# A third buffer for the second layer's input, an earlier load, and a moved stage plan

## Chip, cores and metric

The kernel runs on one core of one Trainium2 chip. The metric is device microseconds of one execution. Engines are named as the profile names them: PE (TensorE), PEld (its weight loads), DVE (VectorE), ACT (ScalarE), POOL (GpSimd) and SP (SyncE), whose only work here is to issue DMA transfers. All data are float32.

## What is computed

Two residual layers over `x` of 8 batches, 1024 tokens and 512 channels, conditioned by `cond` (8 x 1024). Cut to what matters:

```python
# layer 0: modulated attention, 16 heads of 32
xn  = layernorm(x * s1)                      # s1, s2: the halves of cond
q, k, v = xn @ Wq.T * q_dc, xn @ Wk.T * k_dc, xn @ Wv.T * v_dc * s2
out = softmax(q @ k.T * scale) @ v
x   = x + out @ Ww.T * w_dc + v @ Wu.T * u_dc

# layer 1: gated state-space scan, 1024 inner channels, 16 states
xr, gate = split(x @ W_in.T)                 # 1024 columns each
xr  = xr + cond
xc  = silu(causal_conv4(xr) + b_conv)        # depthwise over tokens, 4 taps
xn  = (xc - mean) / sqrt(var + 1e-5) * ln_g + ln_b
Bm, Cm, dt = split(xn @ W_xproj.T)           # 16 columns each
Ad  = 1 - tanh(dt @ W_dt.T + b_dt) * 0.01 * tanh(A_log)
Bd  = Bm * min(norm(xn), 1)
for t in range(1024):                        # h: 8 x 16 x 1024
    h = clip(h * Ad[t] + Bd[t] * xn[t], -10, 10)
    y[t] = Cm[t] @ h
x   = x + ((y + D * xn) * silu(gate)) @ W_out.T
```

## The kernel before

**The whole.** `modulated_attention` does layer 0 and leaves its result in a DRAM scratch `x1_d`, cut into 32 chunks of 32 tokens (512 KB a chunk, all batches). `gated_scan` does layer 1. All instructions stand in each engine's queue in the order in which Python emits them (`manual_schedule`), and every engine works through its own queue in that order, waiting on semaphores.

**The scan.** State `h` is one tile of 128 partitions (8 batches x 16 states) by 1024 channels. One token is one `step`: a single custom DVE instruction (L805) that adds the token's weighted input and clamps. Its input is `xb`, the normalised row of the token repeated over the 16 states. It is made by DMA: `spill` writes the normalised tile `xt` (16 tokens, 512 KB) to a DRAM scratch `xd` (L623), and `fetch` reads 4 tokens of it back with 8 broadcast transfers (one a batch, 256 KB landed each, L771). The pool `xbp` holds three such groups of four tokens. `weigh` (ACT, L781) multiplies a token's `xb` by its weight `ws` two steps before its `step`. `products` (PE, L792) sums the states for four tokens into `y`.

**The plan.** Everything else of the layer is cut into small stages and hung on the steps by hand. `at(n, f, ...)` says that stage `f` is emitted right after step `n`. For chunk `c`, `p0 = 32*(c-1)`, so its stages at `p0 - 22` to `p0 + 31` come before its own first step at `p0 + 32`, and those up to `p0 + 84` after it. In a steady stretch every window of 32 steps holds stages of four chunks. Below, "place k" is what is emitted after step k of such a window (k from 0 to 31, so a stage at `p0 - 9` is at place 23). Within a place, earlier chunks come first, then stages in the order of the `at` lines, then `fetch`, `products` and `weigh`.

**The stages of one chunk**, in the order in which its data passes them:

- `load_x1` (SP, L435): the chunk's 512 KB from `x1_d` into `x1`, from a pool of two buffers. A buffer is free when `order(1)` (ACT, L699) of the chunk two back has read it.
- `begin` (ACT): carries three tokens of conv history over.
- `conv_mm` (PE, L546, L550), `conv_in` (ACT, L557, L559), `conv_taps` (DVE, L566), `conv_out` (ACT, L573): input product, conv and silu, eight times, once for each 128 channels, a new one every second step.
- `flip_mm` (PE), `stats`, `center`, `deviation`, `scale` (mostly DVE): transposes and layer norm, for each half of the chunk (tile 0 and tile 1, 16 tokens each); then `spill` (SP) and `squares` (ACT). `skip` (DVE, L636) later scales the same `xt` in place by `D`, so it waits until the spill has read it.
- `p_mm`, `p_out`, `p_flip`, `lengths`, `params`, `params_mm`, `params_out`: the projections Bm, Cm, dt. `spread` (POOL, L667) sends them with 8 small transfers to the 128 partitions as `bca`; `decay` (ACT tanh L671, then DVE) makes the weights `ws` and the clamp limits from them, `weights` (DVE) the matrices for `products`.
- `order`, `gate_mm` (PE, L704), `gate` (ACT, L712), `add_y`, `gate_y` (DVE, L717, L721), `out_flip`, `out_copy`, `out_mm` (PE, L738, L744), `out_store` (ACT), `out_send` (POOL, L759): the gate and the output product.

**Queues.** SP's queue holds, for one chunk, 64 transfers of `fetch`, two of `spill` and one of `load_x1`. In the built program they take turns on eight semaphores: each SP transfer also waits until the transfer eight places ahead of it in the queue has landed. All matrix results of the layer share four PSUM buffers (tag `mm`), two more hold `y`.

Of the kernel before, what the change touches and what calls it, by code (L numbers as in the profile page):

```python
# [8 lines left out]
F32 = mybir.dt.float32  # L9
# [6 lines left out]
P = 128  # L16
B = 8
H = 512
KH = H // P
# [3 lines left out]
KI = DI // P  # L23
NS = 16
TC = 32
# [3 lines left out]


@with_exitstack
def modulated_attention(ctx, tc, const, x1_d, xu_d, S, x, xT, cond, wT, ident, sT):

# [5 lines left out]
    nc = tc.nc  # L41
# [3 lines left out]
    SB = 2 * NQ  # L45
    NAMES = ("q", "k", "v", "w", "u")

    eps = const.tile([P, 1], F32, name="eps_h")
    nc.vector.memset(eps, EPS)
    dc = const.tile([P, 5, KH, B], F32, name="dc")  # L50
    xp = ctx.enter_context(tc.tile_pool(name="xh", bufs=3))
    tok = ctx.enter_context(tc.tile_pool(name="tok", bufs=2))
    small = ctx.enter_context(tc.tile_pool(name="small", bufs=6))
# [59 lines left out]
    with tc.tile_pool(name="w0", bufs=2) as wp:  # L113
        s2T = wp.tile([P, 2 * KH, B], F32, name="s2T")
        nc.scalar.activation(s2T, sT, AF.Square)
        for n, name in enumerate(NAMES):
            w = wp.tile([P, KH, H], F32, name="w")
# [21 lines left out]
    two = ctx.enter_context(tc.tile_pool(name="two", bufs=2))  # L139
# [259 lines left out]
def gated_scan(ctx, tc, const, x1_d, S, w_in, w_conv, cols, ln_g, ln_b, w_x, w_xd, w_dt, b_dt, a_log,  # L399
# [10 lines left out]
    nc = tc.nc  # L410
# [3 lines left out]
    NX = 3 * NS  # L414

    wp = ctx.enter_context(tc.tile_pool(name="w1", bufs=1))
    one = ctx.enter_context(tc.tile_pool(name="s1", bufs=1))
    two = ctx.enter_context(tc.tile_pool(name="s2", bufs=2))
    hp = ctx.enter_context(tc.tile_pool(name="hp", bufs=6))
    xcp = ctx.enter_context(tc.tile_pool(name="xcp", bufs=2))  # L420
    xtp = ctx.enter_context(tc.tile_pool(name="xtp", bufs=4))
# [6 lines left out]
    def load(ap, name, shape):  # L428
        t = wp.tile(shape, F32, name=name)
        nc.sync.dma_start(out=t, in_=ap)  # L430
        return t

    def load_chunk(c):
        x1 = two.tile([P, KH, B, TC], F32, name="x1")
        nc.sync.dma_start(  # L435
            out=x1.rearrange("p k b t -> p (k b t)"), in_=x1_d[c].rearrange("p k b t -> p (k b t)")
        )
        return x1

    win_sb = wp.tile([P, KH, 2 * DI], F32, name="win")  # L440
    nc.sync.dma_start(out=win_sb[:, :, 0:DI], in_=w_in[:, 0:DI].rearrange("(k p) o -> p k o", p=P))
    x1_now = load_chunk(0)
    cw = load(w_conv.rearrange("(k p) j -> p k j", p=P), "cw", [P, KI, 4])
    cb = load(cols["b_conv"], "cb", [P, KI])
    lg = load(cols["ln_g"], "lg", [P, KI])
    lb = load(cols["ln_b"], "lb", [P, KI])
    g_bc = load(ln_g.unsqueeze(0).to_broadcast([P, DI]), "g_bc", [P, DI])
    b_bc = load(ln_b.unsqueeze(0).to_broadcast([P, DI]), "b_bc", [P, DI])
    d_bc = load(d_skip.unsqueeze(0).to_broadcast([P, DI]), "d_bc", [P, DI])
# [6 lines left out]
    nc.sync.dma_start(out=wx_sb[:, :, 0 : 2 * NS], in_=w_x.rearrange("(k p) o -> p k o", p=P))  # L456
    wxd = xtp.tile([NS, DI], F32, tag="xt", name="wxd")
    nc.sync.dma_start(out=wxd, in_=w_xd)
    wdt = load(w_dt, "wdt", [NS, NS])
    my_sb = load(mask_y, "mask_y", [P, B])  # L460

    few = wp.tile([P, 4 * CW], F32, name="few")
# [6 lines left out]
    eps = wp.tile([P, 1], F32, name="eps_i")  # L469
    nc.vector.memset(eps, EPS)  # L470
    nc.scalar.activation(na, na, AF.Tanh)
    nc.vector.tensor_scalar_mul(na, na, -0.01)
    zero = wp.tile([P, TC], F32, name="zero")
    nc.vector.memset(zero, 0.0)

# [21 lines left out]
    pts = []  # L499
    for n in range(2):  # L500
        pt = wp.tile([P, 2 * NS + P], F32, name=f"pt{n}")
        nc.vector.memset(pt, 0.0)
        pts.append(pt)
    yws = []
    for n in range(2):
        yw = wp.tile([P, TT, 4 * B], F32, name=f"yw{n}")
# [23 lines left out]
    def at(n, f, *args):  # L530
        plan.setdefault(n, []).append(lambda: f(*args))
# [4 lines left out]
    def load_x1(st, c):  # L536
        st["x1"] = load_chunk(c)
# [106 lines left out]
    def params(st, i):  # L644
        rs = st["rs", i]
        pt = st["p", i] = pts[i][:, 0:NX]
        add = two.tile([P, NX], F32, name="p_add")
        nc.vector.scalar_tensor_tensor(add, wgs, rs[:, 1:2], wb, ALU.mult, ALU.add)
        nc.vector.scalar_tensor_tensor(pt, st["pt_ps"][:, i, 0:NX], rs[:, 0:1], add, ALU.mult, ALU.add)
        nc.vector.tensor_scalar_mul(pt[:, 0:NS], pt[:, 0:NS], st["nr"][:, i : i + 1])  # L650
# [161 lines left out]
    for c in range(NCH):  # L812
        st, n0 = sts[c], c * TC
        p0 = n0 - TC
        if c > 0:
            at(p0 + -15, load_x1, st, c)
        at(p0 + -15, begin, st)
        for k in range(KI):
            at(p0 + -9 + 2 * k, conv_mm, st, k)
            at(p0 + -8 + 2 * k, conv_in, st, k)  # L820
            at(p0 + -7 + 2 * k, conv_taps, st, k, (0, 1))
            at(p0 + -6 + 2 * k, conv_taps, st, k, (2,))
            at(p0 + -5 + 2 * k, conv_out, st, k)
        at(p0 + 11, flip_mm, st, 0, 0)
        at(p0 + 11, flip_mm, st, 0, 1)
        at(p0 + 12, stats, st, 0, 0)
        at(p0 + 12, stats, st, 0, 1)
        at(p0 + 12, center, st, 0)
        at(p0 + 13, deviation, st, 0)
        at(p0 + 14, scale, st, 0)  # L830
        at(p0 + 15, spill, st, 0)
        at(p0 + 17, squares, st, 0)
        at(p0 + 23, skip, st, 0)
        at(p0 + 14, flip_mm, st, 1, 0)
        at(p0 + 14, flip_mm, st, 1, 1)
        at(p0 + 15, stats, st, 1, 0)
        at(p0 + 15, stats, st, 1, 1)
        at(p0 + 15, center, st, 1)
        at(p0 + 16, deviation, st, 1)
        at(p0 + 17, scale, st, 1)  # L840
        at(p0 + 22, spill, st, 1)
        at(p0 + 18, squares, st, 1)
        at(p0 + 28, skip, st, 1)
        at(p0 + 15, p_mm, st)
        at(p0 + 19, p_out, st)
        at(p0 + 20, p_flip, st)
        at(p0 + 18, lengths, st)
        at(p0 + 22, params, st, 0)
        at(p0 + 23, params_mm, st, 0)
        at(p0 + 24, params_out, st, 0)  # L850
        at(p0 + 20, params, st, 1)
        at(p0 + 21, params_mm, st, 1)
        at(p0 + 24, params_out, st, 1)
        at(p0 + 25, spread, st)
        at(p0 + 29, decay, st)
        at(p0 + 30, weights, st, 0)
        at(p0 + 36, weights, st, 1)
        at(p0 + 31, order, st, 0)
        at(p0 + 38, gate_mm, st, 0, 0)
        at(p0 + 40, gate, st, 0, 0)  # L860
        at(p0 + 41, gate_mm, st, 0, 1)
        at(p0 + 42, gate, st, 0, 1)
        at(p0 + 51, add_y, st, 0)
        at(p0 + 56, gate_y, st, 0)
        at(p0 + 59, out_flip, st, 0, 0)
        at(p0 + 60, out_copy, st, 0, 0)
        at(p0 + 62, out_mm, st, 0, 0)
        at(p0 + 60, out_flip, st, 0, 1)
        at(p0 + 62, out_copy, st, 0, 1)
        at(p0 + 65, out_mm, st, 0, 1)  # L870
        at(p0 + 68, out_store, st, 0)
        at(p0 + 70, out_send, st, c, 0)
        at(p0 + 48, order, st, 1)
        at(p0 + 51, gate_mm, st, 1, 0)
        at(p0 + 54, gate, st, 1, 0)
        at(p0 + 54, gate_mm, st, 1, 1)
        at(p0 + 58, gate, st, 1, 1)
        at(p0 + 65, add_y, st, 1)
        at(p0 + 73, gate_y, st, 1)
        at(p0 + 75, out_flip, st, 1, 0)  # L880
        at(p0 + 76, out_copy, st, 1, 0)
        at(p0 + 78, out_mm, st, 1, 0)
        at(p0 + 75, out_flip, st, 1, 1)
        at(p0 + 77, out_copy, st, 1, 1)
        at(p0 + 79, out_mm, st, 1, 1)
        at(p0 + 81, out_store, st, 1)
        at(p0 + 82, out_send, st, c, 1)
    for g in range(S // 4):
        at(4 * g - 9, fetch, g)
        at(4 * g + 4, products, g)  # L890
# [13 lines left out]
@with_exitstack  # L904
def network(ctx: ExitStack, tc: tile.TileContext, S, ins, out):
    nc = tc.nc
    const = ctx.enter_context(tc.tile_pool(name="const", bufs=1))
    dram = ctx.enter_context(tc.tile_pool(name="dram", bufs=1, space=DRAM))
    x1_d = dram.tile([S // TC, P, KH, B, TC], F32, name="x1_d")
    xu_d = dram.tile([2, H, S], F32, name="xu_d")  # L910
    ident = const.tile([P, P], F32, name="ident")
    nc.sync.dma_start(out=ident, in_=ins["ident"])
    sT = const.tile([P, 2 * KH, B], F32, name="sT")
    nc.sync.dma_start(out=sT, in_=ins["condT"].rearrange("(k p) b -> p k b", p=P))
    with tc.manual_schedule():
        modulated_attention(
            tc, const, x1_d, xu_d, S, ins["x"], ins["xT"], ins["cond"], {n: ins[f"w{n}T"] for n in "qkvwu"}, ident, sT
        )
        gated_scan(
            tc, const, x1_d, S, ins["w_in"], ins["w_conv"],  # L920
            {n: ins[f"{n}_c"] for n in ("b_conv", "ln_g", "ln_b")}, ins["ln_g"], ins["ln_b"],
            ins["w_x"], ins["w_xd"], ins["w_dt"], ins["b_dt"], ins["a_log"], ins["d_skip"],
            ins["w_out"], ident, ins["cond_k"], ins["mask_y"], out,
        )
# [65 lines left out]
```

## Time and profile before

| | |
|---|---|
| median of 3 runs | 6010.15 us (6007.41 to 6031.06) |
| the profiled execution's own time | 6021.71 us |
| its span, first to last instruction | 6019.9 us |
| layer 0 | about 0 to 3465 us |
| second layer's constants and first chunk | about 3465 to 3549 us |
| scan, first to last step | 3549 to 5997 us |
| busy in the whole span | PE 94%, DVE 74%, ACT 64%, POOL 26% |
| granted TensorE clock, mean | 0.98 |

The engines' rows of the profile give busy time; idle time before an instruction is put down to what released it. DMA share is the mean busy share of the core's 16 DMA engines. A queue line of SP shows when a transfer was issued, not when it landed.

### The profile page before, as it was taken

The numbers are of one execution on the slowest core, as the hardware profiler recorded it, in microseconds if no ns is written. First come the engines' busy times: TensorE is split into PE (matmuls) and PEld (weight loads), VectorE is DVE, ScalarE is ACT, GpSimd is POOL, SyncE is SP. The second block draws the span as 40 slices with busy tenths as digits, with TensorE's granted clock in tenths as the row PEclk, the third lists the DMA queues.
The fourth block names the chain that finished last, engine by engine and source line by source line (L and its number), as shares of the span: only waits on it lengthen the run. The fifth ranks groups of instructions, "written<-read, shape, count | busy, mean of one in ns | idle before, by whom it ended". The sixth has DMA issues, their size and how long they took to land.

```text
span 6019.9 us, 113426 instructions
## 1 busy us (share of the span) xinstructions
PE 5660.1 (94%) x42960; PEld 3310.4 (55%) x42960; DVE 4469.2 (74%) x6917; ACT 3846.8 (64%) x6743; POOL 1549.8 (26%) x1668
## 2 busy tenths in 40 slices
PE   7999999999999999999999879999999999999998
PEld 5555555555555555555555545555555555555553
DVE  2666666766666666667666569999989998989997
ACT  3655555655655555556555358877777777777786
POOL 2433433433433434334333201101111111111111
PEclk8999999999999999999999989999999999999999
DMA  2102212111112022121111279999989999899997
GB/s 71 38 17 64 52 41 64 29 57 50 37 48 66 21 59 59 34 64 37 51 37 36 63 203 252 248 244 248 249 239 246 248 250 243 241 242 247 241 249 207
DMA packets 387648, 781.81 MB, mean 130 GB/s; under 512 B 203664, under 2 KB 285840, under 8 KB 354336
## 3 DMA queue, kind: packets, MB, share of 16 engines
q1 hardware_dynamic: 358432, 756.07, 46.2%
q0 software_dynamic: 28672, 18.48, 1.4%
q8 instruction: 342, 5.60, 0.4%
q14 instruction: 202, 1.65, 0.1%
HBM read 663.62 MB, written 83.89 MB: 124 GB/s over the span
## 4 chain that ended last, share of the span: by engine, by line
PE 51%; DMA 27%; DVE 8%; ACT 8%; SPq 4%; issue 2%; POOL 0%; ACTq 0%; DVEq 0%; POOLq 0%
DMA xb<-xd 24%; PE mm_ps L153 16%; PE t_ps L262 13%; PE s_ps L252 9%; PE mm_ps L269 8%; DVE h L805 4%; SPq L771 4%; ACT pr L370 3%; ACT pT L367 2%; PE in_ps L546 1%; DMA xd<-xt 1%; ACT xb L781 1%; DVE xt L604 1%; PE y_ps L792 1%; PE o_ps L744 1%
## 5 line engine op out<-in xcount | busy, mean ns | idle before, releaser
L360 DVE TENSOR_REDUCE nmax<-s_ps 128x1 f32<-128x1024 f32 x1024 | 1206.1, 1220 | 478.2 <-PE s_ps L255 477.6
L367 ACT COPY pT<-t_ps 128x512 f32<-128x512 f32 x1024 | 550.1, 589 | 1377.7 <-PE t_ps L262 1377.4
L805 DVE CUSTOM_DVE_ANT_0 h<-h,xb,lim 128x1024 f32<-128x1024 f32 x1024 | 1372.9, 1341 | 64.4 <-ACT xb L781 21.0
L262 PEld LDWEIGHTS t_ps<-ident,pr 128*128 128x128 f32 x8192 | 910.0, 141 | 647.0 <-issue 451.3
L781 ACT ACTIVATE xb<-xb,ws 128x1024 f32<-128x1024 f32 x1024 | 1152.4, 1146 | 174.6 <-DMA xb<-xd 151.8
L370 ACT ACTIVATE pr<-s_ps,nmax 128x1024 f32<-128x1024 f32 x1024 | 1140.3, 1128 | 5.7 <-DVE nmax L360 5.5
L262 PE MATMUL t_ps<-ident,pr 128*128 128x128 f32 x8192 | 1095.9, 277 | 30.8 <-ACT pT L367 28.5
L546 PE MATMUL in_ps<-x,win 128*128 128x256 f32 x2048 | 530.2, 405 | 88.0 <-DMA x<-x_d 88.0
L389 POOL TENSOR_SCALAR pr<-pr,rinv 128x1024 f32<-128x1024 f32 x512 | 575.2, 1123 | 144.7 <-DVE rinv L388 140.8
L252 PE MATMUL s_ps<-kT,qT 32*128 32x512 f32 x2048 | 601.0, 641 | 4.4 <-ACT pr L370 4.4
L255 PE MATMUL s_ps<-k,q 32*128 32x512 f32 x2048 | 578.0, 640 | 0.0
L759 POOL DMA_DIRECT2D out<-o_sb x256 | 150.5, 594 | 1642.5 <-ACT xr L557 824.3
L375 POOL TENSOR_SCALAR pr<-pr,rinv 128x1024 f32<-128x1024 f32 x256 | 287.5, 1123 | 1107.8 <-PE t_ps L262 740.2
L269 PEld LDWEIGHTS mm_ps<-pT,vt 128*32 128x32 f32 x16384 | 438.0, 110 | 235.3 <-issue 94.4
L269 PE MATMUL mm_ps<-pT,vt 128*32 128x128 f32 x16384 | 517.5, 274 | 47.7 <-ACT vt L200 18.6
L792 PE MATMUL y_ps<-h,yw 128*32 128x512 f32 x4096 | 533.5, 610 | 12.4 <-DVE h L805 12.4
L546 PEld LDWEIGHTS in_ps<-x,win 128*128 128x128 f32 x2048 | 397.6, 200 | 248.9 <-issue 120.1
L384 POOL TENSOR_SCALAR pr<-pr,rinv 128x1024 f32<-128x1024 f32 x256 | 287.5, 1123 | 880.8 <-DVE rinv L383 854.0
L704 PE MATMUL g_ps<-win,x1t 128*128 128x512 f32 x1024 | 467.3, 599 | 2.3 <-ACT sq_ps L630 2.3
L744 PE MATMUL o_ps<-wout,xt 128*128 128x512 f32 x1024 | 463.7, 596 | 0.1
L566 DVE SCALAR_TENSOR_TENSOR xc<-xr,cw,xc 128x256 f32<-128x256 f32 x768 | 369.5, 481 | 94.6 <-ACT xc L559 81.4
L381 DVE COPY pT<-t_ps 128x512 f32<-128x512 f32 x512 | 352.1, 688 | 77.2 <-PE t_ps L262 76.8
(131 smaller groups left out, 6830.7 us busy)
## 6 DMA issues: line engine op xcount, KB each, us to landing
xb<-xd SPq DMA_DIRECT2D x2048, 256.0 KB
xd<-xt SPq DMA_DIRECT2D x64, 512.0 KB
xq<-in_x SPq DMA_DIRECT2D x16, 1024.0 KB
q<-qT SPq DMA_DIRECT2D x128, 128.0 KB
xr<-in_xT SPq DMA_DIRECT2D x64, 256.0 KB
xu_d<-xr SPq DMA_DIRECT2D x64, 256.0 KB
xr<-xu_d SPq DMA_DIRECT2D x64, 256.0 KB
x_d<-xr SPq DMA_DIRECT2D x64, 256.0 KB
```

The costliest lines, as they stand in the source:

```text
L153: nc.tensor.matmul(ps, w, x, start=(k == 0), stop=(k == KH - 1))
L252: nc.tensor.matmul(s_ps[i][:, 0:HW], st["q"][r, qc], st["k"][r, 0:HW], start=True, stop=True)
L255: nc.tensor.matmul(s_ps[i][:, HW:S], st["q2"][r, qc], st["k2"][r], start=True, stop=True)
L262: nc.tensor.transpose(ps[:, j], pr[:, c0 : c0 + P], ident)
L269: nc.tensor.matmul(av[r], vt[:, kt, r], pT[:, i, kt], start=(kt == 0), stop=(kt == KT - 1), skip_group_check=True,)
L360: nc.vector.tensor_reduce(nmax[i], s_ps[i], AX.X, ALU.max, negate=True)
L367: nc.scalar.copy(pT[:, 0, 4 * g : 4 * g + 4], t_ps[g])
L370: nc.scalar.activation(fresh[i], s_ps[i], AF.Exp, bias=nmax[i], accum_out=rsum[i])
L546: nc.tensor.matmul(ps, win_sb[:, kk, k * P : (k + 1) * P], st["x1"][:, kk].rearrange("p b t -> p (b t)"), start=(kk == 0), stop=False,)
L781: nc.scalar.mul(xbs[n], xbs[n], sts[c]["ws"][:, t : t + 1])
L792: nc.tensor.matmul(st["y", i][32 * r : 32 * r + 32, hf * 512 : (hf + 1) * 512], yws[i][:, 4 * q + r, :], hs[4 * g + r][:, hf * 512 : (hf + ...
L805: nc.vector._custom_dve(dve_ops.TENSOR_ADD_SAT, out=h, in0=last["h"], in1=xbs.pop(n), s0=lim[:, 0, t : t + 1], s1=lim[:, 1, t : t + 1],)
```

## The change

It does three things. `x1` gets a third buffer and its load is issued at `p0 - 22` instead of `p0 - 15`; the first product `conv_mm(0)` goes from `p0 - 9` to `p0 - 8`, so the load stands fourteen steps ahead of it instead of six. To make room in SBUF (4 KB a partition), layer 0's condition and coefficient tiles move to a pool that ends with that layer, three small constants of layer 1 lie in a tile pool's buffers that are used again later, a tile of zeros becomes a view of another tile's zero columns, and `p_add` has one buffer instead of two. And about fifty stages of the plan move by one to four steps (the first `gate` by four).

```diff
-        x1 = two.tile([P, KH, B, TC], F32, name="x1")
+        x1 = two.tile([P, KH, B, TC], F32, bufs=3, name="x1")
...
-    lg = load(cols["ln_g"], "lg", [P, KI])
-    lb = load(cols["ln_b"], "lb", [P, KI])
+    lgb = xtp.tile([P, 2, KI], F32, tag="xt", name="lgb")
...
-    wdt = load(w_dt, "wdt", [NS, NS])
+    wdt = xtp.tile([NS, NS], F32, tag="xt", name="wdt")
...
-    zero = wp.tile([P, TC], F32, name="zero")
-    nc.vector.memset(zero, 0.0)
+    zero = pts[0][:, NX : NX + TC]
...
-        add = two.tile([P, NX], F32, name="p_add")
+        add = one.tile([P, NX], F32, name="p_add")
...
-            at(p0 + -15, load_x1, st, c)
-        at(p0 + -15, begin, st)
+            at(p0 + -22, load_x1, st, c)
+        at(p0 + -14, begin, st)
         for k in range(KI):
-            at(p0 + -9 + 2 * k, conv_mm, st, k)
-            at(p0 + -8 + 2 * k, conv_in, st, k)
-            at(p0 + -7 + 2 * k, conv_taps, st, k, (0, 1))
-            at(p0 + -6 + 2 * k, conv_taps, st, k, (2,))
-            at(p0 + -5 + 2 * k, conv_out, st, k)
+            at(p0 + -8 + 2 * k, conv_mm, st, k)
+            at(p0 + -7 + 2 * k, conv_in, st, k)
+            at(p0 + -6 + 2 * k, conv_taps, st, k, (0, 1))
+            at(p0 + -5 + 2 * k, conv_taps, st, k, (2,))
+            at(p0 + -4 + 2 * k, conv_out, st, k)
...
-        at(p0 + 15, spill, st, 0)
-        at(p0 + 17, squares, st, 0)
-        at(p0 + 23, skip, st, 0)
+        at(p0 + 16, spill, st, 0)
+        at(p0 + 16, squares, st, 0)
+        at(p0 + 27, skip, st, 0)
...
-        at(p0 + 22, spill, st, 1)
-        at(p0 + 18, squares, st, 1)
+        at(p0 + 20, spill, st, 1)
+        at(p0 + 19, squares, st, 1)
...
-        at(p0 + 19, p_out, st)
-        at(p0 + 20, p_flip, st)
-        at(p0 + 18, lengths, st)
+        at(p0 + 17, p_out, st)
+        at(p0 + 19, p_flip, st)
+        at(p0 + 19, lengths, st)
...
-        at(p0 + 24, params_out, st, 0)
+        at(p0 + 25, params_out, st, 0)
...
-        at(p0 + 24, params_out, st, 1)
+        at(p0 + 22, params_out, st, 1)
         at(p0 + 25, spread, st)
-        at(p0 + 29, decay, st)
-        at(p0 + 30, weights, st, 0)
-        at(p0 + 36, weights, st, 1)
+        at(p0 + 30, decay, st)
+        at(p0 + 32, weights, st, 0)
+        at(p0 + 34, weights, st, 1)
...
-        at(p0 + 40, gate, st, 0, 0)
-        at(p0 + 41, gate_mm, st, 0, 1)
-        at(p0 + 42, gate, st, 0, 1)
-        at(p0 + 51, add_y, st, 0)
+        at(p0 + 44, gate, st, 0, 0)
+        at(p0 + 43, gate_mm, st, 0, 1)
+        at(p0 + 44, gate, st, 0, 1)
+        at(p0 + 52, add_y, st, 0)
         at(p0 + 56, gate_y, st, 0)
-        at(p0 + 59, out_flip, st, 0, 0)
-        at(p0 + 60, out_copy, st, 0, 0)
-        at(p0 + 62, out_mm, st, 0, 0)
-        at(p0 + 60, out_flip, st, 0, 1)
-        at(p0 + 62, out_copy, st, 0, 1)
+        at(p0 + 57, out_flip, st, 0, 0)
+        at(p0 + 58, out_copy, st, 0, 0)
+        at(p0 + 61, out_mm, st, 0, 0)
+        at(p0 + 58, out_flip, st, 0, 1)
+        at(p0 + 60, out_copy, st, 0, 1)
...
```

The stages of the gate and output of tile 1 move in the same way: `order` 48 to 47, `gate_mm` 51 and 54 to 50 and 55, `gate` (first half) 54 to 53, `add_y` 65 to 67, `gate_y` 73 to 71, `out_flip` 75 to 73, `out_copy` 76 and 77 to 74, `out_send` 82 to 84; of tile 0, `out_store` goes from 68 to 67 and `out_send` from 70 to 68.

More of the change, by code (lines that the diff above doesn't have):

```diff
@@ L31, in modulated_attention @@
 @with_exitstack
-def modulated_attention(ctx, tc, const, x1_d, xu_d, S, x, xT, cond, wT, ident, sT):
+def modulated_attention(ctx, tc, const, x1_d, xu_d, S, x, xT, cond, wT, ident, condT):
     nc = tc.nc
@@ L46, in modulated_attention @@
     NAMES = ("q", "k", "v", "w", "u")
-    eps = const.tile([P, 1], F32, name="eps_h")
+    own = ctx.enter_context(tc.tile_pool(name="own", bufs=1))
+    sT = own.tile([P, 2 * KH, B], F32, name="sT")
+    nc.sync.dma_start(out=sT, in_=condT.rearrange("(k p) b -> p k b", p=P))
+    eps = own.tile([P, 1], F32, name="eps_h")
     nc.vector.memset(eps, EPS)
-    dc = const.tile([P, 5, KH, B], F32, name="dc")
+    dc = own.tile([P, 5, KH, B], F32, name="dc")
     xp = ctx.enter_context(tc.tile_pool(name="xh", bufs=3))
@@ L444, in gated_scan @@
     cb = load(cols["b_conv"], "cb", [P, KI])
-    lg = load(cols["ln_g"], "lg", [P, KI])
-    lb = load(cols["ln_b"], "lb", [P, KI])
+    lgb = xtp.tile([P, 2, KI], F32, tag="xt", name="lgb")
+    lg, lb = lgb[:, 0], lgb[:, 1]
+    nc.sync.dma_start(out=lg, in_=cols["ln_g"])
+    nc.sync.dma_start(out=lb, in_=cols["ln_b"])
     g_bc = load(ln_g.unsqueeze(0).to_broadcast([P, DI]), "g_bc", [P, DI])
@@ L458, in gated_scan @@
     nc.sync.dma_start(out=wxd, in_=w_xd)
-    wdt = load(w_dt, "wdt", [NS, NS])
+    wdt = xtp.tile([NS, NS], F32, tag="xt", name="wdt")
+    nc.sync.dma_start(out=wdt, in_=w_dt)
     my_sb = load(mask_y, "mask_y", [P, B])
@@ L870, in gated_scan @@
-        at(p0 + 65, out_mm, st, 0, 1)
[L871 to L876, printed above, removed]
+        at(p0 + 57, out_flip, st, 0, 0)
[3 more added lines that the diff above has]
+        at(p0 + 60, out_copy, st, 0, 1)
+        at(p0 + 65, out_mm, st, 0, 1)
@@ L877, in gated_scan @@
+        at(p0 + 67, out_store, st, 0)
+        at(p0 + 68, out_send, st, c, 0)
+        at(p0 + 47, order, st, 1)
+        at(p0 + 50, gate_mm, st, 1, 0)
+        at(p0 + 53, gate, st, 1, 0)
+        at(p0 + 55, gate_mm, st, 1, 1)
         at(p0 + 58, gate, st, 1, 1)
[L878 to L881, printed above, removed]
+        at(p0 + 67, add_y, st, 1)
+        at(p0 + 71, gate_y, st, 1)
+        at(p0 + 73, out_flip, st, 1, 0)
@@ L882, in gated_scan @@
+        at(p0 + 74, out_copy, st, 1, 0)
         at(p0 + 78, out_mm, st, 1, 0)
-        at(p0 + 75, out_flip, st, 1, 1)
-        at(p0 + 77, out_copy, st, 1, 1)
+        at(p0 + 73, out_flip, st, 1, 1)
+        at(p0 + 74, out_copy, st, 1, 1)
         at(p0 + 79, out_mm, st, 1, 1)
         at(p0 + 81, out_store, st, 1)
-        at(p0 + 82, out_send, st, c, 1)
+        at(p0 + 84, out_send, st, c, 1)
     for g in range(S // 4):
@@ L912, in network @@
     nc.sync.dma_start(out=ident, in_=ins["ident"])
-    sT = const.tile([P, 2 * KH, B], F32, name="sT")
-    nc.sync.dma_start(out=sT, in_=ins["condT"].rearrange("(k p) b -> p k b", p=P))
     with tc.manual_schedule():
         modulated_attention(
-            tc, const, x1_d, xu_d, S, ins["x"], ins["xT"], ins["cond"], {n: ins[f"w{n}T"] for n in "qkvwu"}, ident, sT
+            tc, const, x1_d, xu_d, S, ins["x"], ins["xT"], ins["cond"], {n: ins[f"w{n}T"] for n in "qkvwu"}, ident, ins["condT"]
         )
```

## The prediction

> **What bounds the kernel now.** I read the page first, for where the time lies, then the busy times by stretch, then the waits of the second layer, then the timelines of PE and SP over one chunk.
>
> ```profile
> span 6019.9 us, 113426 instructions
> ...
> DMA  2102212111112022121111279999989999899997
> GB/s 71 38 17 64 52 41 64 29 57 50 37 48 66 21 59 59 34 64 37 51 37 36 63 203 252 248 244 248 249 239 246 248 250 243 241 242 247 241 249 207
> ```
>
> The change touches only the last 2450 us, where DMA is busy for the first time. There, three resources stand close to full:
>
> ```profile
> core 0: us, PE busy (x) PEld busy (x) DVE busy (x) ACT busy (x) POOL busy (x), PEclk, DMA share, GB/s
> ...
> 4500.00:5000.00 500.00, 470.43 (x2226) 258.24 (x2225) 458.08 (x651) 392.32 (x675) 58.81 (x108) 0.99 0.90 246
> ```
>
> PE 94%, DVE 92%, DMA 90%, ACT 78%. The group row of the scan step in 3600 to 5900 us gives the pace: 952 steps in 2300 us, 2.416 us a step, **77.3 us a chunk**.
>
> ```profile
> L805 DVE CUSTOM_DVE_ANT_0 h<-h,xb,lim 128x1024 f32<-128x1024 f32 x952 | 1276.3, 1341 | 48.0 <-DMA xb<-xd 12.9 <-ACT xb L781 12.6 <-PE y_ps L792 8.6
> ```
>
> Who waits, in the same 2300 us (about 30 chunks):
>
> ```profile
> ACT xr L557 <- PE in_ps L550: 185.2, 92, 4.1
> ...
> ACT xb L781 <- DMA xb<-xd: 122.6, 62, 3.8
> ...
> PE in_ps L546 <- DMA x<-x_d: 85.7, 30, 4.1
> DVE xc L566 <- ACT xc L559: 69.5, 43, 3.3
> ...
> DVE xt L636 <- DMA xd<-xt: 35.8, 21, 4.1
> ```
>
> Read it as a chain: once a chunk (30 times) PE has nothing to do until `x1` lands, 2.86 us on average; then ACT waits for PE's product, and DVE for ACT. Twice a chunk (62 times) ACT waits for broadcast tokens, and `skip` waits for a spill. PE around that place:
>
> ```profile
> 4521.61 0.49 PE L655 MATMUL xp_ps<-ident,pt 128*128 128x128 f32 x3
> 4525.89 1.97 PE L546 MATMUL in_ps<-x,win 128*128 128x256 f32 x8 [3.79 <-DMA x<-x_d]
> ```
>
> One chunk earlier, and the busy times of two microseconds there (the 0.50 is the granted clock):
>
> ```profile
> 4446.84 3.75 PE L546 MATMUL in_ps<-x,win 128*128 128x256 f32 x8 [3.86 <-DMA x<-x_d]
> ```
>
> ```profile
> 4446.00:4448.00 2.00, 1.16 (x3) 1.01 (x4) 2.00 (x2) 2.00 (x7) 0.00 (x0) 0.50 0.73 188
> ```
>
> The gap has a second price: there the same product took 3.75 us instead of 1.97. The trace's clock record has 22 such spells of 3.4 or 6.8 us between 3560 and 5950 us, nearly all starting within 5 us of that gap; without what falls into the gap itself, half of them is 51 us of PE time, 1.7 us a chunk.
>
> Why the load is late is in SP's queue:
>
> ```profile
> 4503.29 0.56 SPq L623 DMA_DIRECT2D xd<-xt  x1
> 4504.55 10.35 SPq L771 DMA_DIRECT2D xb<-xd  x8
> 4515.45 0.32 SPq L435 DMA_DIRECT2D x<-x_d  x1
> 4516.51 9.73 SPq L771 DMA_DIRECT2D xb<-xd  x8
> 4526.90 0.57 SPq L623 DMA_DIRECT2D xd<-xt  x1
> ```
>
> The load (place 17) stands behind the spill and fetch of place 15. That fetch needed 10.35 us to issue instead of about 5, since its last transfer waits for the spill, eight places ahead. The load went out at 4515.45, PE wanted it at 4522.1. DMA runs empty and full in turn over the same stretch:
>
> ```profile
> 4504.00:4508.00 4.00, 4.00 (x17) 2.95 (x17) 3.86 (x7) 2.00 (x4) 0.00 (x0) 1.00 0.43 102
> ...
> 4526.00:4532.00 6.00, 6.00 (x35) 3.82 (x36) 5.16 (x8) 4.59 (x11) 4.04 (x8) 1.00 0.57 161
> ...
> 4540.00:4582.00 42.00, 42.00 (x193) 22.75 (x192) 41.05 (x65) 35.29 (x60) 2.38 (x4) 1.00 0.99 262
> ```
>
> The lulls follow the two spills; full, it moves 262 GB/s.
>
> **The change part by part**, for one chunk.
>
> *The load of x1.* Same 512 KB, same one transfer. It goes to place 10, between the fetches of places 7 and 11, and with three buffers it no longer waits for `order(1)` at place 16. PE asks for it at place 24, 14 steps or over 30 us later, against the 10.4 us it needed here. Removed from PE: 2.86 us of idling and, with the gap, the half clock, 1.7 us. It passes the fetches of places 11 and 15: its 0.5 MB takes 2.0 us at 262 GB/s from the first. That one feeds the steps from 20 on, which ACT wants at place 18, over 10 us after; hidden. Were it not, ACT would wait up to 2.0 us there.
>
> *The spills.* Spill 0 goes from ahead of the fetch of place 15 to behind it, at place 16, when SP is otherwise waiting for step 19. Spill 1 goes from place 22 (right ahead of a fetch) to 20 (behind the fetch of place 19). So neither holds the last transfer of the next fetch for its 10 us. I expect the lulls to close, and most of ACT's 122.6 us and `skip`'s 35.8 us of waits to go: `skip(0)` also moves from place 23 to 27. New risk: the fetch of place 23 needs spill 0 landed. Issued near 4511 to 4514 on the clock above, plus 11.4 us (the spill in the chain of waits), it lands at 4522 to 4526; step 23, which that fetch waits for anyway, ends about 4522.5. Cost 0 to 3 us, taken as 0.5; the before had such waits too.
>
> *Conv one step later*, all eight, with `begin`. Order on PE is kept (`params_mm`, `conv_mm(0)`, `products`). Only the last `conv_out` comes nearer to `flip_mm` at place 11. DVE gives 3 steps (about 4.3 us) for 0.86 us of silu and 1 us of transposes. Hidden, if PE is level; otherwise up to 1 us.
>
> *p_out and p_flip.* PE's gaps of 0.87 us (`p_flip` waiting for ACT's copy) should go, `p_out` now being two places ahead. `add_y(0)`, 1.2 us, now stands ahead of `params(1)` on DVE, and PE's next wait, 0.42 us here, grows by about that. Sum 0, bounds minus 0.9 to plus 1.2.
>
> *decay to place 30, params_out(0) to 25.* `spread` follows `params_out(0)`. Its landing:
>
> ```profile
> DMA to landing us min/median/max: 4.9/8.3/10.7
> ```
>
> With PE's gap gone the road to `decay` is shorter. From the start of `conv_mm(0)`: three copies (1.3 us), eight issues (4.1), landing (8.3): 13.7 us. ACT gets to its tanh after two further products and their neighbours on PE (10.1 us), a conv_in (0.95) and a weigh (1.15): 12.2 us. ACT and DVE stand about 1.5 us (0 to 3.9 over the landings seen). Queued behind the tanh are `conv_out(1)`, the first `weigh` of the next chunk (which needs `decay`'s result) and `conv_in(3)`. But PE has `out_mm(0,0)` (4.7 us) and `conv_mm(3)` (2.4) to do until about 19 us. I take 0.4. This is what I expect late next.
>
> *Gate and output stages*: same instructions, no new short wait on PE, except `out_flip(0)` one place behind `gate_y(0)`; the 4.3 us of `conv_mm(0)` and `products` cover its 2.6 us. DVE gets six pairs of steps with nothing between instead of three, 0.17 us each: plus 0.5. *Setup* (constants, zeros, pools): same transfers, one memset fewer, run once; 0, within 5 us either way.
>
> **The sum.** What each resource needs a chunk:
>
> - PE: 77.3 - 2.9 - 1.7 = 72.7.
> - DVE: 458.08/500 of 77.3 = 70.8, plus bubbles (0.17 each, six) and small unmoved waits, 1.3: 72.1.
> - DMA: 246 GB/s times 77.3 us = 19.0 MB; at 262 GB/s 72.6.
>
> For the last there is a rule that would let it drop out. The Trainium skill, "DMA: Bandwidth & Descriptors", section "Measured (HBM→SBUF, 128 partitions, SWDGE, issued from GpSimd)", measures 341 GB/s for transfers of 1 MB. By it (an estimate) DMA would need 55.7 us and bound nothing. The row at share 0.99 says 262 for these broadcasts; the row decides. And a rule speaks against the change: "SBUF — State Buffer", section "Can I just issue two DMAs to hit both halves?", says that all DMAs share the same 16 engines. So the earlier load adds no capacity; alone, at 246 of 262 GB/s, it could save 4.7 us a chunk at most.
>
> All three stop at 72 to 73 us. Three in-order queues at 98% do not meet without loss: I add 0.4 and 0.5 from above and 0.3 for local mismatch, to 72.7: **73.9**, 3.4 us less. Over 28 full chunks (the first ones run at 74 to 75 already) 95 us. From the profiled 6021.7 that leaves 5926.7; times 6010.15/6021.71, **5915**.
>
> **The rivals.**
>
> *DMA is the bound as it stands* (0.20). Closing the lulls only makes each transfer slower: for it speaks that its mean, 246 GB/s, is near the full 262, and that the chain of waits from 4500 to 4600 us is 46% broadcast transfer; against, that PE and DVE show waits that are not its. A chunk takes 76 us: 1.3 x 28 = 36, **5973**.
>
> *Nothing is lost to mismatch* (0.13): 72.3 us a chunk, 140 us: **5870**.
>
> *decay takes the place of the wait, and it gets slower* (0.11). Fuller DMA engines delay the tiny `spread` transfers. Up to a landing of 13.6 us PE's 19 us cover it; from there each microsecond is lost on ACT, DVE and PE together. The gain is eaten at 17.0 us; at 18.2, 1.2 x 28 = 34 us are lost: **6045**. Against: 10.7 is the longest seen, at full DMA.
>
> *It does not do what it says* (0.04): SP reaches place 10 so late that the load lands as before: **6010**.
>
> **How the numbers follow.** The main case has 0.52, range 5885 to 5950. A difference of 0.5% (30 us) is about what a measurement of this kernel can tell from none. Faster: 0.52 + 0.13 and 0.12 of the second case; same: its other 0.08 and 0.04; slower 0.11. Range 5860 to 5985, leaving out the slow case and tails.
>
> **What would show it.** PE's wait for `x1` near 0 and the clock at 1.00 all through the scan; ACT's wait for `xb` under 50 us; no DMA stretch of 4 us under 0.6; a chunk near 74 us; `bca` waits grown to 30 to 60 us. I am wrong if the x1 wait is gone and the chunk still takes 76 us or more, or if the wait stays.

## The result, and the profile after

The changed kernel takes 5972.43 us (median of 5 runs), the kernel before 6024.03 us beside it: a ratio of **0.9921 [0.9900, 0.9943]**. The forecast was 5915. The sign held, the size was half: in the profiled executions a chunk of the scan went from 77.3 to 75.4 us (mean of 28 chunks), not to 73.9. From its first step to its last the scan took 2447.8 us before and 2397.8 after, 50.0 us less. The first step comes 3.4 us later (3552.5 us instead of 3549.1), so setup is no part of the gain, and the two executions lie 46.6 us apart.

The busy time by stretch, same columns as before:

```profile
core 0: us, PE busy (x) PEld busy (x) DVE busy (x) ACT busy (x) POOL busy (x), PEclk, DMA share, GB/s
...
4500.00:5000.00 500.00, 483.59 (x2294) 264.63 (x2287) 467.44 (x677) 403.87 (x692) 58.86 (x108) 0.99 0.94 252
```

PE rose from 94% to 97%, DMA from 246 to 252 GB/s, where the prediction had 262 for full engines. The first product in the groups of 3560 to 5860 us (busy, mean ns, idle before it):

```profile
L551 PE MATMUL in_ps<-x,win 128*128 128x256 f32 x1928 | 455.6, 379 | 0.0
```

The wait for `x1` is gone: 85.7 us of idling before, 0.0 now, and the product takes 379 ns on average instead of 404. Time at half clock (3560 to 5840 us, from the trace's clock record) fell from 112.6 to 47.8 us. The other waits of the same stretch (total, times, longest):

```profile
ACT xb L786 <- DMA xb<-xd: 123.6, 96, 3.4
ACT xr L562 <- PE in_ps L555: 82.8, 72, 2.8
PE xp_ps L660 <- DVE pt L655: 63.3, 30, 3.5
DVE xt L641 <- DMA xd<-xt: 50.7, 25, 3.6
ACT bca L676 <- DMA bca<-few: 16.9, 10, 3.9
```

The first and the fourth line decide. ACT waits for broadcast tokens as long as before (125.7 us in the same stretch), and `skip` waits longer for the spill (35.8 before). SP itself, whose queue also waits for spills to land, waits longer than before. Its lines in the kernel before and in the change:

```profile
SPq L771 <- DMA xd<-xt: 188.1, 60, 5.1
```

```profile
SPq L776 <- DMA xd<-xt: 222.8, 60, 5.3
```

The queue shows it in one chunk of the change:

```profile
4646.55 0.57 SPq L628 DMA_DIRECT2D xd<-xt  x1
4649.29 9.23 SPq L776 DMA_DIRECT2D xb<-xd  x8
4659.02 0.57 SPq L628 DMA_DIRECT2D xd<-xt  x1
```

Both spills are at their new places. The fetch behind the first still needs 9.23 us to issue: its eighth transfer goes out at 4658.04, when the spill has landed, 11.5 us after its issue. And the lulls are still there; after the second spill:

```profile
4658.00:4662.00 4.00, 4.00 (x28) 2.08 (x27) 3.78 (x4) 3.12 (x7) 2.46 (x5) 1.00 0.48 141
4668.00:4670.00 2.00, 2.00 (x21) 1.16 (x11) 0.72 (x1) 2.00 (x5) 0.00 (x0) 1.00 0.35 125
```

### The profile page after: what moved, and what is told of

It reads as the page before. It is cut to its first block, busy times and chain, and to the rows that moved or that the text cites. A ratio compares the mean times of both kernels' runs of the same rounds, so it can differ in the third digit from the quotient of the medians.

```text
span 5973.3 us, 113397 instructions
## 1 busy us (share of the span) xinstructions
PE 5653.9 (95%) x42960; PEld 3294.2 (55%) x42960; DVE 4456.9 (75%) x6916; ACT 3851.8 (64%) x6743; POOL 1545.8 (26%) x1668
## 4 chain that ended last, share of the span: by engine, by line
PE 50%; DMA 29%; ACT 8%; DVE 8%; issue 2%; SPq 2%; POOL 0%; DVEq 0%; ACTq 0%; POOLq 0%
DMA xb<-xd 24%; PE mm_ps L156 16%; PE t_ps L265 13%; PE s_ps L255 9%; PE mm_ps L272 8%; DVE h L810 4%; ACT pr L373 3%; DMA xd<-xt 2%; ACT pT L370 2%; SPq L776 2%; DMA x<-x_d 1%; DVE xc L571 1%; ACT xb L786 1%; PE in_ps L551 1%; DVE nmax L363 0%
## 5 line engine op out<-in xcount | busy, mean ns | idle before, releaser
L797 PE MATMUL y_ps<-h,yw 128*32 128x512 f32 x4096 | 558.2, 601 | 34.8 <-DVE h L810 28.7
L709 PE MATMUL g_ps<-win,x1t 128*128 128x512 f32 x1024 | 488.2, 621 | 1.3 <-DVE xt L609 1.1
L551 PE MATMUL in_ps<-x,win 128*128 128x256 f32 x2048 | 486.2, 380 | 0.0
```

The lines of the kernel that those rows point to most:

```text
L551: nc.tensor.matmul(ps, win_sb[:, kk, k * P : (k + 1) * P], st["x1"][:, kk].rearrange("p b t -> p (b t)"), start=(kk == 0), stop=False,)
```

## The experiments

The experiments set two theories against each other. **D** (in two expectations **B**): full DMA engines set the pace at some 262 GB/s, and the change could only win what the lulls had left; the prediction's first rival is of this kind. **R**, later **S**: the spill is slow to land, and what stands behind it pays, wherever it is put. The first four expectations also have **P**: the wait for `x1` was on the path. Why the spill is slow came last: experiment 7 tests the order in which it writes its rows. All ratios, with 95% intervals, are the recorded ones to the kernel before, run beside each kernel; they are not the quotients of the medians. Where an expectation speaks of a spill on SP's queue landing after about 15 us, that number is wrong: it comes from waiting for sixteen landing records where such a spill has five, so that records of the next transfer were counted. By its own records it is 11 to 12 us, as the prediction's chain of waits had it.

**1. Each half of the change alone.** `x1_only` has the third buffer and the load at `p0 - 22`, with the old plan; `plan_only` the new plan with two buffers and the load at `p0 - 15`.

```diff
# x1_only, against the changed kernel: the plan of before, but
             at(p0 + -22, load_x1, st, c)
# plan_only, against the changed kernel
-        x1 = two.tile([P, KH, B, TC], F32, bufs=3, name="x1")
+        x1 = two.tile([P, KH, B, TC], F32, name="x1")
-            at(p0 + -22, load_x1, st, c)
+            at(p0 + -15, load_x1, st, c)
```

> The third buffer and the load at p0 - 22 alone, all other stages where they were before. Before runs at 77.2 us a chunk, the changed kernel at 75.5. Theory D (the broadcast stream is the bound: what PE no longer waits for x1 it waits for elsewhere): PE's wait for x1 goes from 2.9 us a chunk to 0, ACT's wait for xb grows, a chunk takes 76 us or more, and less than 30 us of the time is gained. Theory P (the x1 wait was on the path and the moved stages give part of it back): this one alone gains as much as the whole change (about 50 us) or more, 75.5 us a chunk or less.

> The moved stages alone: two buffers for x1, its load at p0 - 15, seven steps ahead of the first product. Theory D: the spills' new places do the work, half of the gain or more (25 us or more) is here. Theory P: the x1 wait is still there (about 2 us a chunk) and the moves by themselves bring nothing or cost up to 30 us.

Measured: `x1_only` 5971.01 us, 0.9929 [0.9911, 0.9948]; `plan_only` 5959.94, 0.9904 [0.9888, 0.9921]. Each half brings what both bring. They take away the same thing: in the first no wait of PE for `x1` is left in the list, and in the second it falls to 34.3 us of 85.7, although the load stands where it stood. Neither touches what is left: ACT's waits for `xb` are 143.5 and 111.2 us. Of the forecasts, P's came true for `x1_only` and D's for `plan_only`, so the pair settles nothing between them.

**2. A quarter less to broadcast.** `fetch` brings three tokens of four, from before and from after; the fourth is weighed from the third's row.

```diff
-                out=xb[rows(b)].rearrange("p r c -> p (r c)"),
-                in_=src.unsqueeze(0).to_broadcast([NS, 4 * DI]),
+                out=xb[rows(b)].rearrange("p r c -> p (r c)")[:, 0 : 3 * DI],
+                in_=src[0 : 3 * DI].unsqueeze(0).to_broadcast([NS, 3 * DI]),
...
-        nc.scalar.mul(xbs[n], xbs[n], sts[c]["ws"][:, t : t + 1])
+        nc.scalar.mul(xbs[n], xbs[n - 1 if n % 4 == 3 else n], sts[c]["ws"][:, t : t + 1])
```

> The changed kernel with a quarter of the broadcast left out: each fetch brings three of four tokens, the fourth takes its input from the third (this part of the result is another one). Engines do the same work. Theory D: DMA carries 14.8 instead of 19.0 MB a chunk, ACT no longer waits for xb, a chunk falls to 73 us or less: at least 75 us less than the changed kernel. Theory P: the chunk stays within 1 us of 75.5, since PE's wait at params_mm (2.1 us) and the waits of DVE do not come from DMA.

> The kernel before with the same quarter of the broadcast left out. Theory D: the x1 load lands in time too, and a chunk falls to 74 us or less, so that before and after come to lie within 20 us of each other. Theory P: the wait for x1 shrinks but the plan of before keeps a chunk at 75 us or more.

Measured: 5896.78 us (0.9803 [0.9784, 0.9822]) and 5905.16 (0.9814 [0.9796, 0.9832]); chunks of 73.6 and 73.8 us. DMA matters, and with less of it the change is worth almost nothing. But at 202 GB/s and a share of 0.71 the engines are not full, and still a chunk stays 1.0 us above what experiment 5 reaches with all the bytes. This fits S as well as D.

**3. Two small moves that the profile after suggests.** `skip(1)` later, so that it doesn't wait for its spill; `add_y(0)` back to its old place, out of the way of `params(1)`, for which PE waits 63.3 us (12.7 before); both together with `plan_only`; and, with three buffers and the new plan, the load back at `p0 - 15`.

```diff
-        at(p0 + 28, skip, st, 1)
+        at(p0 + 33, skip, st, 1)          # after_skip, plan_skip_addy
-        at(p0 + 52, add_y, st, 0)
+        at(p0 + 51, add_y, st, 0)         # after_addy, plan_skip_addy
-            at(p0 + -22, load_x1, st, c)
+            at(p0 + -15, load_x1, st, c)  # after_load17
```

> The changed kernel with skip of tile 1 moved from p0 + 28 to p0 + 33, so that DVE asks later for the landing of spill 1, for which it waits 1.8 us a chunk. If that wait is on the path: about 1.5 us a chunk less, 45 us. If DMA sets the pace (theory D): DVE's wait goes and comes back as waits for xb; less than 15 us.

> The changed kernel with add_y of tile 0 back at p0 + 51, ahead of params(1) by a step, as before. PE's wait at params_mm was 0.44 us a chunk before and is 2.1 us now. If it is on the path: about 1.2 us a chunk less, 35 us. Theory D: the wait shrinks to about 1 us and the time stays within 15 us of the changed kernel.

> The moved stages with two buffers and the load at p0 - 15, with skip of tile 1 at p0 + 33 and add_y of tile 0 at p0 + 51. The best version in hand if the small waits add up: 5945. Theory D: within 10 us of 5960.

> The changed kernel with its three buffers, but the load at p0 - 15 (place 17) again. If the third buffer itself did anything, this is like the changed kernel (5972); if only the place of the load matters, like the moved stages alone (5960). Theory D: both within 12 us of 5966, PE waits about 1 us a chunk for x1 and the time does not show it.

Measured: 0.9915 [0.9899, 0.9930], 0.9925 [0.9910, 0.9941], 0.9916 [0.9902, 0.9930], 0.9908 [0.9892, 0.9924]. None differs from the change itself. In `after_skip` the wait of `skip` for the spill is gone from the list and the time stays, so that wait is off the path. `after_addy` is weaker: PE's wait for `params` only fell from 63.3 to 52.3 us, so the move of `add_y(0)` explains little of it. On the new plan neither the third buffer nor the earlier load is worth anything.

**4. The spill on another queue.** If only its turn among SP's eight semaphores hurts, POOL's queue cures it.

```diff
-        nc.sync.dma_start(out=st["xd", i].rearrange("n r c -> r n c"), in_=st["xt", i])
+        nc.gpsimd.dma_start(out=st["xd", i].rearrange("n r c -> r n c"), in_=st["xt", i])
```

> The changed kernel with both spills issued by POOL instead of SP, so that they no longer take a turn among SP's eight semaphores; places, bytes and engines' work as they are. Theory R (part of the missing gain is lost because the slow spill holds up the transfer eight places behind it): the DMA lulls after the spills close, ACT's wait for xb falls from 124 us to under 70, a chunk falls from 75.5 to about 74, 40 us less in all. Theory B (it is the rate of the full DMA engines alone): the same bytes at the same rate, within 12 us of the changed kernel.

> The same on top of the moved stages with two buffers and the load of x1 at p0 - 15 (5960 us). Theory R: about 74 us a chunk or less, 30 us less than without. Theory B: within 12 us of 5960.

Measured: slower, 6069.91 us (1.0092 [1.0066, 1.0118]) and 6136.9 (1.0199 [1.0182, 1.0217]). The DMA issues of the first (KB each, median us to landing) and its waits:

```profile
xd<-xt POOLq DMA_DIRECT2D x58, 512.0 KB, 15.7
bca<-few POOLq DMA_DIRECT2D x240, 6.0 KB, 9.6
```

```profile
POOL bca L672 <- DMA xd<-xt: 119.1, 21, 16.4
ACT bca L676 <- DMA bca<-few: 110.6, 23, 10.2
```

The spill lands later still, and now `spread` stands behind it: ACT waits 110.6 us for `bca`, 16.9 in the change. The move costs more than the turns; it says nothing on how the spill could be quick.

**5. The same bytes in other pieces, and more bytes.** `after_split` writes the spill as four transfers, one for each row index `r`; `plan_more` is `plan_only` with one more load of 512 KB a chunk into a tile that nobody reads.

```diff
# after_split
-        nc.sync.dma_start(out=st["xd", i].rearrange("n r c -> r n c"), in_=st["xt", i])
+        for r in range(4):
+            nc.sync.dma_start(out=st["xd", i][:, r], in_=st["xt", i][32 * r : 32 * r + 32])
# plan_more, against plan_only
+            at(p0 + 1, load_more, c)      # x1_d[c] into an unread tile
```

> The changed kernel with each spill cut into four transfers of 128 KB (one for each of the four rows of a token group), in SP's queue as before. Theory R (the long landing of the spill, which holds the transfer eight places behind it, costs part of the gain): each part lands sooner, the lulls shrink, 20 to 40 us less than the changed kernel. Theory D without R: within 12 us. If the four extra turns among the eight semaphores hurt: 20 us more.

> The moved stages with two buffers and the load at p0 - 15 (5960 us), plus one more load of the same 512 KB a chunk into a tile that nobody reads, issued at p0 + 1, away from the spills and the x1 load. Nothing waits for it. Theory D (the rate of the full DMA engines is what a chunk is made of): 0.5 MB at about 260 GB/s is 2.0 us a chunk, 55 to 65 us more in all. If DMA had room: under 15 us more.

Measured: `after_split` **5887.24 us, 0.9784 [0.9770, 0.9798]**, a chunk 72.5 us. `plan_more` 6008.73, 0.9991 [0.9982, 0.9999]: 49 us more than `plan_only`. The second result is what D expects. The first is 85 us less than the change, twice what R expected at most: not one byte less, and the same plan runs 1.4% faster. That breaks the rival's 76 us a chunk. A bound at 262 GB/s it doesn't break: with the lulls closed, DMA runs at just that rate. Below are the 1400 us from 4000 to 5400, first of the change, then of `after_split`:

```profile
4000.00:5400.00 1400.00, 1349.89 (x6370) 735.64 (x6369) 1301.42 (x1878) 1129.35 (x1925) 159.74 (x292) 0.99 0.94 251
```

```profile
4000.00:5400.00 1400.00, 1367.19 (x6633) 760.88 (x6632) 1350.31 (x1944) 1170.77 (x2002) 166.09 (x304) 1.00 0.99 261
```

The quarters write the same DRAM rows as the whole, each at the same distance of four rows (16 KB), so where the rows lie in DRAM is not what makes the whole slow.

**6. The quarters without the change, and halves.** The same edit on the kernel before, on `x1_only` and on the new plan with two buffers; and the change with the spill in two halves of two row indices each.

```diff
# after_split2
-        for r in range(4):
-            nc.sync.dma_start(out=st["xd", i][:, r], in_=st["xt", i][32 * r : 32 * r + 32])
+        for r in range(0, 4, 2):
+            nc.sync.dma_start(
+                out=st["xd", i][:, r : r + 2].rearrange("n r c -> r n c"), in_=st["xt", i][32 * r : 32 * r + 64]
+            )
```

> The kernel before with each spill cut into four transfers of 128 KB. Theory S (the slow spill is what made the x1 load late and left DMA idle; the change only went partly round it): PE's wait for x1 falls under 1 us a chunk, DMA share over 0.97, within 15 us of 5887. Theory L (the load behind a full fetch is late in any case): PE still waits 2 us or more a chunk for x1, 5930 to 5960.

> Third buffer and load at p0 - 22 on the stage plan of before, spills cut in four. If the moved stages still count: 20 us or more above 5887. Theory S: within 12 us of it, and of before_split.

> Moved stages, two buffers, load at p0 - 15, spills cut in four. If the early load still counts: PE waits 1 us or more a chunk for x1 and it is 15 us or more above 5887. Theory S: within 12 us of it.

> The changed kernel with each spill cut into two transfers of 256 KB. If the landing goes with the transfer's size (15 us whole, 6 us for a quarter), about 9 us: half of the effect or more, 5910 to 5935. If it is the number of turns on SP's semaphores that counts and not the landing: near 5972.

Measured: `before_split` **5871.87 us, 0.9761 [0.9747, 0.9774]**; `x1_split` 5875.65, 0.9764 [0.9751, 0.9778]; `plan_split` 5884.55, 0.9783 [0.9769, 0.9796]; `after_split2` 6253.82, 1.0390 [1.0375, 1.0405]. So the best version is the kernel before with a two-line edit, and with it nothing of the change is left to win: the third buffer gives no difference, the new plan costs some 13 us. Halves are far worse than the whole, where 5910 to 5935 us (by size) or 5972 (by turns) was expected, so neither size nor turns is it. SP and PE in `before_split`, the same part of a chunk:

```profile
4665.75 1.91 SPq L624 DMA_DIRECT2D xd<-xt  x4
4668.44 6.44 SPq L772 DMA_DIRECT2D xb<-xd  x8
4674.99 0.51 SPq L435 DMA_DIRECT2D x<-x_d  x1
```

```profile
4684.07 0.49 PE L656 MATMUL xp_ps<-ident,pt 128*128 128x128 f32 x3
4684.39 1.89 PE L546 MATMUL in_ps<-x,win 128*128 128x256 f32 x8
```

The load stands where it stood in the kernel before, behind spill and fetch, with two buffers, and PE doesn't wait for it. The fetch takes 6.44 us to issue, not 10.35. The wait that the change was made for was itself a result of the slow spill. ACT's wait for `xb`, and SP's waits:

```profile
ACT xb L782 <- DMA xb<-xd: 19.5, 12, 4.8
```

```profile
SPq L772 <- DVE xc L566: 386.7, 118, 9.5
SPq L772 <- DMA xb<-xd: 199.7, 392, 2.1
SPq L772 <- DVE h L806: 190.6, 74, 4.5
```

Of the waits for `xd<-xt` 0.2 us is left (222.8 us in the change, 188.1 before), and SP now waits first of all for DVE: the transfers are ahead of the scan.

**7. A store that nobody needs, in two orders.** On `before_split`, 512 KB a chunk from `x1` into a DRAM tile, once in plain row order and once in the order of the old spill. Bytes, size, queue and place are equal.

```diff
+        xe = dr.tile([32, 4, DI], F32, tag="xe", name="xe")
+        nc.sync.dma_start(out=xe.rearrange("n r c -> (n r) c"), in_=st["x1"].rearrange("p k b t -> p (k b t)"))
# store_turned: "n r c -> r n c"
+        at(p0 + 33, store_more, st)
```

> The kernel before with quartered spills (5872 us), plus one store of 512 KB a chunk from the x1 tile to a DRAM scratch that nobody reads, 128 rows of 4 KB in plain order, at p0 + 33. If the order is what makes a spill slow: its packets lie within 3 to 5 us as those of the x1 load do, and the time rises by what 0.5 MB takes at 262 GB/s and no more, 2 us a chunk, 50 to 65 us. If any large store is slow: packets over 8 us or more, DMA share under 0.97, 80 us or more.

> The same store in the order of the spill: row 32 r + n of the tile to DRAM row 4 n + r, r from 0 to 3 in one transfer. If the order is what makes a spill slow: its packets spread over 8 us or more, DMA share falls under 0.97, and it is 25 us or more slower than the store in plain order. If not: within 12 us of it.

Measured: `store_plain` 5870.36 us, 0.9743 [0.9730, 0.9757]; `store_turned` 5914.24, 0.9813 [0.9800, 0.9827]. The order alone costs 0.7%, 44 us. In plain order another half megabyte a chunk costs nothing, where 50 to 65 us had been expected, and DMA moves 270 GB/s:

```profile
4000.00:5400.00 1400.00, 1380.52 (x6666) 763.50 (x6666) 1360.57 (x1954) 1178.32 (x2014) 169.07 (x308) 1.00 1.00 270
```

That ends D: 262 GB/s is no bound of this kernel.

**Why the turned order is slow** can be read from the pages. The trace keeps a landing record each time the semaphore of a transfer is counted up. The pages' packet counts fit one small packet for each DMA engine that reports a transfer's landing. Here they are, in the order the change, `before_split`, `after_split2`, `store_plain`, `store_turned`:

```profile
DMA packets 387647, 781.80 MB, mean 131 GB/s; under 512 B 203664, under 2 KB 285840, under 8 KB 354336
```

```profile
DMA packets 391490, 781.84 MB, mean 133 GB/s; under 512 B 207504, under 2 KB 289680, under 8 KB 358176
```

```profile
DMA packets 387649, 781.82 MB, mean 125 GB/s; under 512 B 203664, under 2 KB 285840, under 8 KB 354336
```

```profile
DMA packets 396098, 798.62 MB, mean 136 GB/s; under 512 B 208016, under 2 KB 290192, under 8 KB 362784
```

```profile
DMA packets 395714, 798.62 MB, mean 135 GB/s; under 512 B 207632, under 2 KB 289808, under 8 KB 362400
```

Look at "under 512 B". Quartering 64 spills adds 3840 packets, 60 a spill: 4 transfers x 16 in place of 4. Halving adds none: 2 x 2 in place of 4. The 32 plain stores add 512, 16 each; the 32 turned ones 128, 4 each. I read that as the number of DMA engines that work on a transfer: the whole spill runs on **4 of the 16**, a half on 2, a quarter on all 16. The trace's landing records, 3560 to 5860 us, say the same (the spread is the mean time from the twelfth to the last of the 16 landings of a `fetch` transfer):

| kernel | transfer, rows | landing records | us to landing, median | spread in `fetch`, us |
|---|---|---|---|---|
| before | spill, [32, 4] | 5 | 11.1 | 3.4 |
| the change | spill, [32, 4] | 5 | 11.5 | 3.2 |
| `before_split` | quarter, [32, 1] | 16 | 5.0 | 0.7 |
| `after_split2` | half, [32, 2] | 3 | 13.5 | 4.5 |
| `store_plain` | store, [128, 1] | 16 | 7.3 | 0.8 |
| `store_turned` | store, [32, 4] | 5 | 11.0 | 1.9 |

One of the 5 (or 3) records comes about 1 us after the issue, before any data; the other 4 (or 2) are the engines'. The Trainium skill has the rule behind these rows ("DMA: Bandwidth & Descriptors", section "Why a DMA increments its semaphore by 16 and not by 1"): a transfer runs on the largest number of engines, up to 16, that divides the size of the slowest dimension of both its access patterns; each engine used counts up the semaphore by one, and the issuing sequencer writes the missing rest at once. In `n r c -> r n c` the slowest dimension is `r`: 4 in the whole, 2 in a half. In a quarter it is the 32 rows `n`, in the plain store the 128 rows. All six rows of the table agree.

The packets in flight confirm it. Of a whole spill's 128 packets of 4 KB in the change, 4 are under way at once for longer than any other number, and at most 5 to 7; of the quarters' up to 19. In `after_split2`, while both halves are out, 2 are under way for 68% of the time and hardly ever more: both halves lie on the same two engines, which fits their being worse than the whole.

The last column is the price for everyone else: a `fetch` transfer has 16 packets and 16 landings, and with a whole spill about, the last four come over 3 us late (in `after_split2` the last two, by 4.2 us). The fetch issued from 4649.29 in the change shows it: twelve landings of its first transfer lie between 4652.40 and 4652.89, the other four between 4655.96 and 4659.00.

## Why the prediction was half right

**The load of x1: right.** PE's wait went from 85.7 us to 0.0, and what it cost the fetches that it passes doesn't show in the time: ACT waits 123.6 us for `xb`, and 99.7 in `after_load17`, where the load has its old place; that is 0.8 us a chunk, with times of 5972 and 5963 us. The wait itself was no independent cost: `before_split` loses it with load and buffers as they were.

**The clock: right for PE, not for the pace.** Half of the 64.8 us less at half clock is 1.2 us of PE time a chunk; the sum had 1.7. Of the 13 half-clock spells left in the change, 12 start within 1.4 us of the end of PE's new wait for `params`. `x1_only`, which has 13.6 us of that wait, has 3.4 us at half clock and still takes 5971 us, so the spells did not set the pace.

**The step that failed: *The spills*.** "So neither holds the last transfer of the next fetch for its 10 us. I expect the lulls to close, and most of ACT's 122.6 us and `skip`'s 35.8 us of waits to go." Measured: SP waits 222.8 us for spills, ACT 123.6 for `xb`, `skip` 50.7, and slices at 0.48 and 0.35 of DMA remain. The reasoning took the spill for an ordinary transfer in a bad place. It occupies a quarter of the engines wherever it stands, and moving it moves the jam along. The mark was in the views of before: stretches at a DMA share of 0.43 and 0.57 while SP had transfers out. They were put down to a late issue alone; work waiting beside idle engines can also mean engines unevenly loaded. The skill's rule above, read against the spill's line `n r c -> r n c`, would have given 4 engines before any run, and the spill's five landing records stood in the trace of before; the prediction looked at neither. What was lost is this term: `after_split`, the change with that one cause removed, runs at 72.5 us a chunk, better than the 73.9 forecast.

**The floor of 72.6 us for DMA: wrong as a floor.** The share of 0.99 at 262 GB/s was read as a stop. `store_plain` passes 270 GB/s without losing time, and a chunk takes 72.1 us. The sum for PE (72.7) and DVE (72.1) was near the truth: in `before_split` they are what is full,

```profile
4000.00:5400.00 1400.00, 1381.35 (x6676) 763.78 (x6678) 1362.78 (x1956) 1180.50 (x2017) 168.94 (x308) 1.00 0.99 264
```

PE 98.7%, DVE 97.3%. The rule of the Trainium skill that all DMAs share the same 16 engines ("SBUF — State Buffer", section "Can I just issue two DMAs to hit both halves?") was used for capacity only; what decided here is the number of engines within one transfer.

**p_out and p_flip: bound exceeded, no cost seen.** PE's wait for `params` rose from 0.44 to 2.1 us a chunk, by more than the 1.2 allowed. The prediction put the growth down to `add_y(0)`; with `add_y(0)` back, `after_addy` still has 1.7, so what makes the wait stays open. With whole spills it doesn't show in the time: `x1_only` has 13.6 us of it in all and is no faster. That it costs the new plan its 13 us once the spill is quick (53.0 us of that wait in `after_split`, 13.2 in `before_split`) fits, and was not tried alone.

**decay: not late next.** `bca` landed sooner, not later:

```profile
DMA to landing us min/median/max: 4.6/6.2/10.3
```

8.3 was the median before; ACT's wait for it fell from 23.9 to 16.9 us.

**The rivals.** "DMA is the bound as it stands" named the time, 5973, and the pace, 76 us. Its mechanism fell in experiments 5 and 7: a number that fits is no cause. "Nothing is lost to mismatch", 72.3 us a chunk, is what both kernels reach with a quartered spill. What stays open is whether the 49 us of `plan_more` are due to the jam alone: its extra load was not tried beside quartered spills, only a store was.

## What to carry to other kernels

When waits lie near a transfer, ask how it is carried before moving it: the slowest dimension of its patterns, its landing records, or the small packets on the page tell how many DMA engines it uses, and a transfer on few of them holds up all others wherever it stands (here `x1`, `xb`, `skip` and the clock). Here four transfers of plain rows in place of one were worth more than the whole change. And if two halves of a change each bring as much as the whole, they remove the same symptom, and the cause is likely elsewhere.

## What was not expected of the hardware

On SP's queue 512 KB landed after 11 us or after 7, by how the rows are ordered and cut: [32, 4] rows of 4 KB on 4 engines took 11.0 to 11.5 us, [128, 1] on 16 took 7.3, four transfers of [32, 1] in `before_split` 7.2 from the first issue to the last landing (5.0 for one), two of [32, 2] 15.8. And the price falls on the others: the mean DMA share of 0.94 in the change looks nearly full, while in its lulls (0.48 and 0.35) most engines have nothing to do and a few hold up every transfer that has a packet on them. On POOL's queue the same spill left 16 landing records (the same section of the skill says that there all 16 engines count, whatever the shape), so they don't tell on how many it ran; it landed after 15.7 us.
